# The first step's preparation without the queued walks, and the last image's ending eight pieces wide

## The chip, the core and the metric

The kernel runs on one core of one Trainium2 chip. Each core has five engines with their own instruction streams: PE (TensorE, matmuls, with PEld its weight loads), DVE (VectorE), ACT (ScalarE), POOL (GpSimd) and SP (SyncE), which here issues every DMA. Engines wait for one another by semaphores. An engine works through its own stream strictly in the order in which the program was written, so an instruction that waits holds back everything behind it on that engine. The metric is the device time of one execution in microseconds (us), the median over several runs.

## What is computed

The input is eight images of 64 x 64 positions with 96 channels. Every image passes through a selective-scan block, a linear attention and a small quantised network:

```
x = x + ss2d(group_norm(x))            # per image
    xz = x @ in_proj ; 3x3 depthwise conv + silu -> xc ; z is the gate
    xs = xc read along two diagonal orders, forwards and backwards (4 directions)
    delta = softplus(...) ; h_t = h_{t-1} * exp(delta_t * A) + delta_t * u_t * B_t ; y_t = h_t . C_t   # 16 states
    y = the four directions put back in place and added ; layer norm ; * silu(z) ; @ out_proj
t = t + attention(layer_norm(t))       # without softmax: one 97 x 97 Gram matrix per image is enough
t = t + ffn(layer_norm(t))             # 96 -> 384 -> 96, operands rounded to 8 bits
```

## The kernel before

**The scan loop.** `run` walks through 128 sections: 8 images, two passes each (`q` 0 forwards, 1 backwards), and 8 sections of 512 positions (`T`) per pass. A section has 16 states, so the main loop has 2048 steps, one section and state each. In one step ACT makes `decay` (L966) and the scaled input `feedT` (L980), PE turns it into `feed` in PSUM (L988, or L990), DVE scans three groups into `h` (L1001), POOL copies the carry (L1017) and multiplies `h` by C (L1022), and PE adds the result into `y` four steps later (L1036). The row of C for a step is a DMA `cc<-crow` (L957), issued four steps ahead into one of five buffers.

**The prologue of a section.** `prologue(m)` makes what the 16 steps of a section need: matmuls from `u` (L878), `rows` (L883), its transpose and `x` (L888, L891), three matmuls with absolute value (L901, L903), exponential and logarithm (L905, L908), four POOL passes (L912 to L917), three matmuls and DVE passes (L920, L922), `du` on POOL (L929), and its transposes and copies (L934, L936). Sections after the first have it spread over the steps of the section before.

**What is put between the steps.** Everything else is written as generators that hand back an engine and an estimated time, and class `Work` places them: `at(tag)` is called at fixed places in a step and lets jobs put instructions into that engine's stream until a credit is used up. Prologues are urgent; the others are jobs, drawn from streams of phases with a width (how many pieces are open at once). `finish(enough)` runs the same machine without a scan loop beside it, until a condition holds. In it every open job moves on by one engine's worth per round, in the order A, V, P, G.

Per image the phases are: `measures` (group norm statistics, 8 pieces), `front` (fetch and norm, L411 to L506; convolution, L536; the `walk` pieces, which read the stored image along the diagonals, L581, transpose, L588, copy, L590, and store the sequence, L593), and after the scans `tail`. `front` of the next image and `tail` of the previous image are placed between the scan steps. Two stretches have no scan beside them:

- *the start*: `finish` runs until the weights are loaded and walks 0 and 1 of the first image are stored; then `bring` loads `u` for two sections, `prologue(0)` is started, and `finish(lambda: not work.urgent)` runs until it is placed. That call places waiting walks too.
- *the end*: after the last step, `tail` of the last image.

**The ending `tail`.** It has three phases. `join`, 8 pieces of 512 positions: load the two directions `y0`, `y1`, the input and the gate (L625, L627, L632); add the two directions on PE with identity matmuls (L640); copy and take statistics (L647, L650, L651); `rsqrt` (two small ACT and seven small POOL instructions); normalise on ACT (L656); transpose and multiply by the gate (L662, L664); out-projection (L668 to L679); copy (L683), store to `mid` (L684), statistics again, normalise on POOL (L695), Gram matrix (L701), transpose (L712), copy and store to `turned` (L715, L717). Then `attention`, one short chain of 97-wide matmuls (L728 to L746). Then `layers`, 8 pieces: load `xaT` and `t` back (L760, L762), matmuls (L765, L770), copy and statistics (L774, L778), normalise on POOL (L785), transpose (L790), three 8-bit matmuls with two ACT passes each (L799 to L802), L805, L810, L815, two POOL additions (L818, L819) and the store (L820). `join` and `layers` run three pieces at a time.

**PSUM and SBUF.** PSUM's eight banks are: three `feed`, two `bank` for the jobs, and `y` over three. When the loop is over the jobs also have the `feed` banks. The scans' SBUF buffers come from one pool that stays open to the end.

Of the kernel before, what the change touches and what calls it, by code (L numbers as in the profile page):

```python
# [13 lines left out]
ALU = mybir.AluOpType  # L14
# [36 lines left out]
@with_exitstack  # L51
def hybrid_block(ctx, tc, x, out, w):


    nc = tc.nc
    NB = x.shape[0]
    const = ctx.enter_context(tc.tile_pool(name="const", bufs=1))
    dram = ctx.enter_context(tc.tile_pool(name="dram", bufs=4, space=DRAM))
    k = weights(tc, const, dram, w)
    pool = ctx.enter_context(tc.tile_pool(name="scan", bufs=1))  # L60
    psum = ctx.enter_context(tc.tile_pool(name="psum", bufs=1, space=PSUM))
    with tc.manual_schedule():

        k.tables = lambda: nc.scalar.preload_act_table_set("natural_log_exp_and_others")
        run(tc, pool, psum, dram, x, out, k, NB)


def weights(tc, const, dram, w):
# [57 lines left out]

    dd = tile("dd", [P, 2, G])
    both = tile("both", [P, G])
    logs = tile("logs", [P, ND, NJ])
    turned = tile("turned", [ND * NJ, P])  # L130

    def loads():

        nc.sync.dma_start(out=logs, in_=w["a_logs"])
# [24 lines left out]
        nc.scalar.copy(turned, v)  # L159
        k.release(ps)  # L160
        rows = dram.tile([ND * NJ, P], F32, tag="logs", name="logs")
        nc.sync.dma_start(out=rows, in_=turned)
        yield SPIN
        for q in range(2):
            for d in range(2):
                for g in range(G):
                    j = (2 * q + d) * NJ + g * (GC // DPT)
                    nc.sync.dma_start(
                        out=k.a_neg[d * GC : (d + 1) * GC, q, g, :],
                        in_=rows[j : j + GC // DPT, :].rearrange("j (i n) -> (j i) n", n=NS),  # L170
                    )
            yield SPIN
# [18 lines left out]
    def layers():  # L191
# [18 lines left out]
        with tc.tile_pool(name="prep", bufs=1, side="right") as prep:  # L210
            w1s = load("w1s", [DM, HID], w["w1"], pool=prep)
            w2s = load("w2s", [P, 3, DM], w["w2"], pool=prep)
            b1s = load("b1s", [P, 3], w["b1"], pool=prep)
# [5 lines left out]
            nc.vector.tensor_copy(k.w1q, w1s, saturate=False)  # L219
            nc.vector.tensor_copy(k.w2q, w2s, saturate=False)  # L220
# [44 lines left out]
class Work:  # L265
# [6 lines left out]
    def __init__(self, banks):  # L272
        self.now = 0
        self.alone = False
        self.urgent, self.jobs, self.streams = [], [], []
        self.free = [(b, -9) for b in banks]
        self.kept = []
        self.long = []
        self.credit = dict.fromkeys(self.PLACES, 0.0)

# [39 lines left out]
    def at(self, tag, place=0):  # L320
        gain, most = self.PLACES[tag]
        self.credit[tag] = min(most, self.credit[tag] + gain)
        for j in self.urgent + self.jobs:
            while not j.done and j.tag == tag:
                if j.ready > (self.now, place) and (j.spin or not self.alone):
                    break
# [42 lines left out]
    def finish(self, enough):  # L369
# [6 lines left out]
        self.alone = False  # L376
        self.credit = dict.fromkeys(self.PLACES, 0.0)


def view(b, p, *dims):  # L380

# [24 lines left out]
    return r, m  # L406


def fetched(nc, pool, x, b, c):
    xt = pool.tile([P, 4, DM], F32, tag="xt", name="xt", bufs=2)  # L410
    nc.sync.dma_start(out=xt, in_=x[b].rearrange("(t p) c -> p t c", p=P)[:, 4 * c : 4 * c + 4, :])  # L411
    return xt

# [54 lines left out]
def front(tc, work, x, k, at, b):  # L468
# [8 lines left out]
    with tc.tile_pool(name=f"f1_{b}", bufs=1, **area) as p1, tc.tile_pool(name=f"f2_{b}", bufs=2, **area) as p2:  # L477
# [16 lines left out]

        def norm(c):

            xt = fetched(nc, p2, x, b, c)
            ps = yield bank(0.45, 4)
            v = channels(nc, k, ps, xt)
            yield act(0.65)  # L500
            nc.scalar.activation(
                xp[0:DM, 1 + 8 * c : 9 + 8 * c, 1 : WW + 1], v.rearrange("p (h w) -> p h w", w=WW),
                AF.Identity, scale=at.norm[:, 0:1], bias=at.norm[:, 1:2],
            )
            work.release(ps)
            normed.add(c)  # L506
# [92 lines left out]
        yield [walk(c) for c in range(NST)], 3  # L599


def tail(tc, work, x, out, k, at, b):

    nc = tc.nc
    area = dict(reuse_waits="tile")
    with tc.tile_pool(name=f"t1_{b}", bufs=1, **area) as p1:
        gram = p1.tile([DM + 1, DM + 1], F32, tag="gram", name="gram")
        grams = [0]

        with tc.tile_pool(name=f"t2_{b}", bufs=2, **area) as p2:  # L610

            joined = set()

            def join(c):
                s = slice(4 * c, 4 * c + 4)

                def tile(name, shape, bufs=2):
                    return p2.tile(shape, F32, tag=name, name=name, bufs=bufs)
# [7 lines left out]
                t = tile("t", [P, 4, DM], 3)  # L626
                nc.sync.dma_start(out=t, in_=x[b].rearrange("(t p) c -> p t c", p=P)[:, s, :])  # L627
                yield "P", 0.0, 4, False
                while c >= 2 and c - 2 not in joined:
# [3 lines left out]
                st, mv = tile("st", [P, 4, 6]), tile("mv", [P, 4, 2])  # L633
                yn = ys[0]
                for j in range(2):
# [21 lines left out]
                yg = tile("yg", [HC, 2, CH])  # L657
                for a in range(2):
                    ps = yield bank(0.45)
                    v = view(ps, HC, CH)  # L660
# [20 lines left out]
                        )  # L681
                yield act(0.5)
                nc.scalar.copy(t, po)  # L683
                nc.sync.dma_start(out=at.mid[:, s, :], in_=t)  # L684
                yield dve(1.7, 0)
                for i in range(4):
                    nc.vector.bn_stats(st[:, i, :], po[:, i, :])
# [25 lines left out]
                xaT = ys[1].rearrange("p a c -> p (a c)")[0 : DM + 1, 0:CH]  # L713
                yield act(0.6)
                nc.scalar.copy(xaT, v)  # L715
                work.release(ps)
                nc.sync.dma_start(out=at.turned[:, c * CH : (c + 1) * CH], in_=xaT)  # L717
                joined.add(c)

            yield [join(c) for c in range(NCH)], 3  # L720

        att = SimpleNamespace()

# [24 lines left out]

        yield [attention()], 1

        with tc.tile_pool(name=f"t3_{b}", bufs=3, **area) as p2:

            def layers(c):
                s = slice(4 * c, 4 * c + 4)
# [4 lines left out]
                xaT = tile("xaT", [DM + 1, CH])  # L759
                nc.sync.dma_start(out=xaT, in_=at.turned[:, c * CH : (c + 1) * CH])  # L760
                t = tile("t", [P, 4, DM])
                nc.sync.dma_start(out=t, in_=at.mid[:, s, :])  # L762
# [56 lines left out]
                nc.gpsimd.tensor_tensor(t, t, y16, ALU.add)  # L819
                nc.sync.dma_start(out=out[b].rearrange("(t p) c -> p t c", p=P)[:, s, :], in_=t)  # L820

            yield [layers(c) for c in range(NCH)], 3


def run(tc, pool, psum, dram, x, out, w, NB):

# [4 lines left out]


    nc = tc.nc
    steps = [
        (b, q, c) for b in range(NB) for q in range(2) for c in (range(NST) if q == 0 else range(NST - 1, -1, -1))
    ]
# [281 lines left out]
    for m in range(2):  # L1120
        bring(m)
    work.start(prologue(0), urgent=True)
    work.finish(lambda: not work.urgent)

    work.kept = feed
    work.finish(lambda: all(any(f is x for x, _ in work.free) for f in feed))
# [17 lines left out]
    for i in range(total + LAG + 1):  # L1144
# [34 lines left out]
        if i + 4 < total:  # L1179
            fetch(i + 4)  # L1180
        feeds.pop(i, None)
    work.free += [(f, -9) for f in feed]
    work.kept = []
    work.stream(end(NB - 1))
    work.finish(all_done)


# [75 lines left out]
```

## Time and profile before

| | us |
|---|---|
| median of 3 runs | 12009.75 (12005.47 to 12027.36) |
| profiled execution, its own time | 12015.44 |
| its span, first to last instruction | 12013.6 |
| first scan instruction (L1001) starts | 308.18 |
| first load of the last image's ending (L625) is issued | 11640.26 |
| busy: PE, DVE, ACT, POOL | 9964.7, 9683.0, 9500.1, 9739.2 |

The busy times are totals over the span. All four engines are busy for about four fifths of it, but not alike everywhere: the first 308 us and the last 373 us have no scan in them, and they must be read on their own. In a line of the timeline the columns are start, duration from the first to the end of the last merged instruction, engine, line, operation, output and input, count, and in brackets the idle time before it with what ended it. In a line of the chain of waits they are start, duration and what was running or being waited for.

### The profile page before, as it was taken

What the parts mean: (1) busy time and instruction counts of PE and PEld (TensorE: products, weight loads), DVE (VectorE), ACT (ScalarE), POOL (GpSimd) and SP (SyncE); (2) the same over time, 40 slices, a digit from 0 to 9 for tenths busy, and PEclk for the clock granted to TensorE, in tenths of its full rate; (3) what the DMA queues carried; (4) which work ended last, traced back from release to release, by engine and by line L of the source; (5) the groups of instructions that cost most, each with busy time, mean ns of one, the idle gap of its engine ahead of it and who ended that gap; (6) DMA issues with size and microseconds to landing.
All of it is one profiled execution on the core that took longest, in us unless ns stands there. A gap on an engine that the chain in (4) does not pass through costs nothing.

```text
span 12013.6 us, 186895 instructions
## 1 busy us (share of the span) xinstructions
PE 9964.7 (83%) x62805; PEld 8013.1 (67%) x62805; DVE 9683.0 (81%) x11092; ACT 9500.1 (79%) x19843; POOL 9739.2 (81%) x6927
## 2 busy tenths in 40 slices
PE   5888889888898888888898888988889888888875
PEld 4676677666676667766676666766667666666653
DVE  1888988888888888888888888888888878888971
ACT  2888888878887788887888778887788878878862
POOL 0879988889878888788988888878898888889972
PEclk8999999998999989999899999989899998988985
DMA  3234333533335333343334433343333533322331
GB/s 98 84 97 129 100 91 89 136 106 101 88 96 143 98 93 95 107 125 103 91 92 128 116 93 90 95 129 109 96 92 92 134 105 94 105 83 82 99 96 39
DMA packets 1126629, 1213.55 MB, mean 101 GB/s; under 512 B 453061, under 2 KB 732326, under 8 KB 1125670
## 3 DMA queue, kind: packets, MB, share of 16 engines
q1 hardware_dynamic: 1125670, 1201.61, 36.4%
q8 instruction: 499, 8.18, 0.3%
q14 instruction: 460, 3.77, 0.1%
HBM read 877.99 MB, written 323.14 MB: 100 GB/s over the span
## 4 chain that ended last, share of the span: by engine, by line
PE 30%; ACT 20%; DVE 20%; POOL 12%; issue 9%; DMA 4%; SPq 3%; DVEq 0%; POOLq 0%; ACTq 0%
DVE h L1001 13%; ACT feedT L980 8%; PE y L1036 7%; PE feed L988 7%; POOL h L1022 7%; ACT decay L966 6%; DVE feed L1005 4%; PE bank L536 3%; DMA cc<-crow 2%; PE bank L878 2%; SPq L581 2%; POOL delta L917 1%; PE bank L920 1%; PE feed L990 1%; PE bank L901 1%
## 5 line engine op out<-in xcount | busy, mean ns | idle before, releaser
L1022 POOL TENSOR_TENSOR h<-h,cc 128x1536 f32<-128x1536 f32 x2048 | 7073.5, 3454 | 390.0 <-DMA cc<-crow 197.1
L1001 DVE TENSOR_TENSOR_SCAN h<-decay,carry,feed 128x512 f32<-128x512 f32 x5376 | 6502.6, 1261 | 635.1 <-PE feed L988 528.8
L966 ACT ACTIVATE decay<-delta,a_neg 128x512 f32<-128x512 f32 x6144 | 3976.2, 713 | 1287.5 <-DVE h L1001 1281.8
L988 PE MATMUL feed<-ident,feedT 128*128 128x128 f32 x15360 | 2746.2, 303 | 1502.8 <-DVE h L1001 1211.3
L1036 PE MATMUL y<-ident,h 128*128 128x128 f32 x24576 | 3806.0, 290 | 72.2 <-ACT ys L1064 40.2
L980 ACT ACTIVATE feedT<-duT,rows 128x192 f32<-128x192 f32 x10240 | 3671.1, 443 | 4.5 <-PE feed L988 3.9
L1036 PEld LDWEIGHTS y<-ident,h 128*128 128x128 f32 x24576 | 3151.0, 151 | 530.5 <-issue 477.3
L988 PEld LDWEIGHTS feed<-ident,feedT 128*128 128x128 f32 x15360 | 1972.3, 155 | 2121.2 <-DVE h L1001 663.5
L1005 DVE TENSOR_TENSOR feed<-feed,du 128x512 f32<-128x512 f32 x2304 | 1442.1, 686 | 209.7 <-PE feed L990 205.2
L1017 POOL COPY carry<-h 128x3 f32<-128x3 f32 x2048 | 395.7, 193 | 1072.5 <-DVE h L1001 959.6
L1001 DVE TENSOR_TENSOR_SCAN h<-decay,feed 128x512 f32<-128x512 f32 x768 | 883.3, 1201 | 95.5 <-PE feed L988 80.4
L536 PE MATMUL bank<-wf,xp 97*128 97x192 f32 x4266 | 864.6, 334 | 1.2 <-DVE delta L922 1.2
L990 PE MATMUL feed<-x,pick 77*128 77x512 f32 x1536 | 848.6, 635 | 0.6
L536 PEld LDWEIGHTS bank<-wf,xp 97*128 97x128 f32 x4266 | 696.0, 195 | 29.6 <-issue 18.5
L922 DVE SCALAR_TENSOR_TENSOR delta<-bank,delta 128x512 f32<-128x512 f32 x383 | 259.7, 678 | 280.8 <-POOL delta L917 144.7
L929 POOL TENSOR_TENSOR du<-delta,u 128x1536 f32<-128x1536 f32 x128 | 449.6, 3513 | 36.1 <-DVE delta L922 36.1
L920 PE MATMUL bank<-x,ws 13*128 13x512 f32 x766 | 444.9, 661 | 17.6 <-DVE delta L922 17.6
L915 POOL TENSOR_TENSOR e<-e,duT 128x1536 f32<-128x1536 f32 x128 | 441.7, 3451 | 14.5 <-ACT delta L908 14.4
L901 PE MATMUL bank<-x,ws 13*128 13x512 f32 x764 | 434.1, 648 | 15.0 <-ACT x L891 15.0
L917 POOL TENSOR_TENSOR delta<-delta,e 128x1536 f32<-128x1536 f32 x128 | 441.2, 3447 | 0.1
L912 POOL TENSOR_SCALAR duT<-e 128x1536 f32<-128x1536 f32 x128 | 193.9, 1514 | 227.8 <-ACT e L905 227.8
L990 PEld LDWEIGHTS feed<-x,pick 77*128 77x128 f32 x1536 | 261.4, 202 | 153.7 <-issue 97.7
(263 smaller groups left out, 9059.9 us busy)
## 6 DMA issues: line engine op xcount, KB each, us to landing
cc<-crow SPq DMA_DIRECT2D x4096, 128.0 KB
u<-seq SPq DMA_DIRECT2D x256, 384.0 KB
wide<-ys SPq DMA_DIRECT2D x512, 192.0 KB
ut<-image SPq DMA_DIRECT2D x768, 64.0 KB
seq<-us SPq DMA_DIRECT2D x128, 384.0 KB
part<-ys SPq DMA_DIRECT2D x64, 768.0 KB
y<-part SPq DMA_DIRECT2D x64, 768.0 KB
y<-wide SPq DMA_DIRECT2D x256, 192.0 KB
```

The costliest lines, as they stand in the source:

```text
L536: nc.tensor.matmul(v[:, j, :], flat[:, o : o + P], k.wf[:, i, :], start=(i == 0), stop=(i == 8), skip_group_check=True)
L901: nc.tensor.matmul(ps, w.ws[:, q, g, :], x[0 : 2 * NR + 1, :], start=True, stop=True)
L917: nc.gpsimd.tensor_tensor(delta, delta, e, ALU.add)
L920: nc.tensor.matmul(ps, w.ws[:, q, g, :], x[0 : 2 * NR + 1, :], start=True, stop=True)
L966: nc.scalar.activation(decays[i][:, g, :], made[m].delta[:, g, :], AF.Exp, scale=w.a_neg[:, q, g, n : n + 1])
L980: nc.scalar.activation(f[part], o.duT[part], AF.Copy, scale=scale)
L988: nc.tensor.transpose(feed[g][:, j * P : (j + 1) * P], feeds[i][:, j * G + g, :], w.ident)
L990: nc.tensor.matmul(feed[0], w.pick[:, FEED[:n].count("D"), :], made[m].x, start=True, stop=True)
L1001: nc.vector.tensor_tensor_scan(h[:, g, back], a[:, g, back], feed[g][:, back], init, ALU.mult, ALU.add)
L1005: nc.vector.tensor_tensor(feed[g], feed[0], made[m].du[:, g, :], ALU.mult)
L1022: nc.gpsimd.tensor_tensor(hs[i], hs[i], c.unsqueeze(1).to_broadcast([P, G, T]), ALU.mult)
L1036: nc.tensor.matmul(y[:, j, :], hs[i][:, g, r * P : (r + 1) * P], w.ident, is_transpose=True, start=(n == 0 and j % 4 == 0), stop=(n == NS ...
```

## The change

It has four parts.

1. A new method `hurry` replaces `finish` for `prologue(0)`: only urgent jobs are placed, and no new pieces are drawn from the streams. Walks 3 to 7 of the first image come later, among the scan steps.
2. The last image's `tail` is called with `last=True`, after the scans' SBUF pool has been closed and the three banks of `y` have been added to the free banks. All phases are eight pieces wide. The two directions are added by one DVE instruction of 128 x 768 instead of PE; the PE additions and the ACT copy after them fall away for this image. `t` and `xaT` stay in SBUF, so the stores to `mid` and `turned` and the loads from them fall away.
3. `norm` in `front` fetches into three buffers instead of two (`measures` keeps two).
4. Some weight tiles move into short-lived memory, and the two bias loads `b1s`, `b2s` are issued after the first three walks' loads instead of before them.

```
@@ class Work
-        for j in self.urgent + self.jobs:
+        for j in self.urgent + ([] if self.hurried else self.jobs):
...
+    def hurry(self, enough):
+        self.alone = self.hurried = True
+        while not enough():
+            self.now += 1
+            for tag, place in (("A", 0), ("V", 0), ("P", 2), ("G", 0)):
+                self.at(tag, place)
+        self.alone = self.hurried = False
@@ norm in front
-            xt = fetched(nc, p2, x, b, c)
+            xt = fetched(nc, p2, x, b, c, 3)
@@ tail
-        with tc.tile_pool(name=f"t2_{b}", bufs=2, **area) as p2:
+        with tc.tile_pool(name=f"t2_{b}", bufs=8 if last else 2, **area) as p2:
...
+                t = p1.tile([P, 4, DM], F32, tag=f"t{c}", name="t") if last else tile("t", [P, 4, DM], 3)
...
+                if last:
+                    yield dve(2.5)
+                    nc.vector.tensor_tensor(yn, ys[0], ys[1], ALU.add)
+                    for i in range(4):
+                        nc.vector.bn_stats(st[:, i, :], yn[:, i, :])
+                        nc.vector.bn_aggr(mv[:, i, :], st[:, i, :])
+                for j in range(0 if last else 2):
...
-                nc.sync.dma_start(out=at.mid[:, s, :], in_=t)
+                if not last:
+                    nc.sync.dma_start(out=at.mid[:, s, :], in_=t)
...
-                nc.sync.dma_start(out=at.turned[:, c * CH : (c + 1) * CH], in_=xaT)
+                if last:
+                    kept[c] = t, xaT
+                else:
+                    nc.sync.dma_start(out=at.turned[:, c * CH : (c + 1) * CH], in_=xaT)
...
-            yield [join(c) for c in range(NCH)], 3
+            yield [join(c) for c in range(NCH)], 8 if last else 3
@@ layers
+                if last:
+                    t, xaT = kept[c]
...
-            yield [layers(c) for c in range(NCH)], 3
+            yield [layers(c) for c in range(NCH)], 8 if last else 3
@@ run
     work.start(prologue(0), urgent=True)
-    work.finish(lambda: not work.urgent)
+    work.hurry(lambda: not work.urgent)
...
-    work.free += [(f, -9) for f in feed]
+    work.finish(all_done)
+    scans.close()
+    y = psum.tile([P, TB * G, P], F32, tag="y", name="y_end").rearrange("p (b k) c -> p b (k c)", b=G)
+    work.free += [(f, -9) for f in feed] + [(y[:, g, :], -9) for g in range(G)]
     work.kept = []
-    work.stream(end(NB - 1))
+    work.stream(tail(tc, work, x, out, w, image(NB - 1), NB - 1, True))
     work.finish(all_done)
```

More of the change, by code (lines that the diff above doesn't have):

```diff
@@ L59, in hybrid_block @@
     k = weights(tc, const, dram, w)
-    pool = ctx.enter_context(tc.tile_pool(name="scan", bufs=1))
     psum = ctx.enter_context(tc.tile_pool(name="psum", bufs=1, space=PSUM))
@@ L64, in hybrid_block @@
         k.tables = lambda: nc.scalar.preload_act_table_set("natural_log_exp_and_others")
-        run(tc, pool, psum, dram, x, out, k, NB)
+        run(tc, psum, dram, x, out, k, NB)
 def weights(tc, const, dram, w):
@@ L128, in weights, with transfers @@
     both = tile("both", [P, G])
-    logs = tile("logs", [P, ND, NJ])
-    turned = tile("turned", [ND * NJ, P])
     def loads():
+        with tc.tile_pool(name="prep", bufs=1, side="right") as prep:
+            yield from transfers(tile("logs", [P, ND, NJ], pool=prep), tile("turned", [ND * NJ, P], pool=prep))
+    def transfers(logs, turned):
         nc.sync.dma_start(out=logs, in_=w["a_logs"])
@@ L212, in layers @@
             w2s = load("w2s", [P, 3, DM], w["w2"], pool=prep)
+            for _ in range(2):
+                yield SPIN
+            nc.vector.tensor_copy(k.w1q, w1s, saturate=False)
+            nc.vector.tensor_copy(k.w2q, w2s, saturate=False)
+        with tc.tile_pool(name="prep", bufs=1, side="right") as prep:
             b1s = load("b1s", [P, 3], w["b1"], pool=prep)
@@ L217, in layers @@
                 yield SPIN
-            nc.vector.tensor_copy(k.w1q, w1s, saturate=False)
-            nc.vector.tensor_copy(k.w2q, w2s, saturate=False)
             s8 = tile("b1e", [P, 3], F8, prep)
@@ L277, in __init__ @@
         self.kept = []
+        self.hurried = False
         self.long = []
@@ L406, in rsqrt, with fetched @@
     return r, m
-def fetched(nc, pool, x, b, c):
-    xt = pool.tile([P, 4, DM], F32, tag="xt", name="xt", bufs=2)
+def fetched(nc, pool, x, b, c, bufs=2):
+    xt = pool.tile([P, 4, DM], F32, tag="xt", name="xt", bufs=bufs)
     nc.sync.dma_start(out=xt, in_=x[b].rearrange("(t p) c -> p t c", p=P)[:, 4 * c : 4 * c + 4, :])
@@ L599, in front, with tail @@
         yield [walk(c) for c in range(NST)], 3
-def tail(tc, work, x, out, k, at, b):
+def tail(tc, work, x, out, k, at, b, last=False):
     nc = tc.nc
@@ L608, in tail @@
         grams = [0]
-        with tc.tile_pool(name=f"t2_{b}", bufs=2, **area) as p2:
+        kept = {}
+        with tc.tile_pool(name=f"t2_{b}", bufs=8 if last else 2, **area) as p2:
             joined = set()
@@ L617, in tile @@
                 def tile(name, shape, bufs=2):
-                    return p2.tile(shape, F32, tag=name, name=name, bufs=bufs)
+                    return p2.tile(shape, F32, tag=name, name=name, bufs=8 if last else bufs)
                 ys = [tile(f"y{d}", [P, 4, DI], 3) for d in range(2)]
@@ L625, in join @@
                         nc.sync.dma_start(out=y[v * WW : (v + 1) * WW], in_=rv)
-                t = tile("t", [P, 4, DM], 3)
+                t = p1.tile([P, 4, DM], F32, tag=f"t{c}", name="t") if last else tile("t", [P, 4, DM], 3)
                 nc.sync.dma_start(out=t, in_=x[b].rearrange("(t p) c -> p t c", p=P)[:, s, :])
-                yield "P", 0.0, 4, False
-                while c >= 2 and c - 2 not in joined:
+                if not last:
+                    yield "P", 0.0, 4, False
+                while not last and c >= 2 and c - 2 not in joined:
                     yield SPIN
@@ L633, in join @@
                 st, mv = tile("st", [P, 4, 6]), tile("mv", [P, 4, 2])
+                yg = tile("yg", [HC, 2, CH]) if last else None
                 yn = ys[0]
-                for j in range(2):
+                if last:
[5 more added lines that the diff above has]
+                for j in range(0 if last else 2):
                     ps = yield bank(0.65)
@@ L656, in join @@
                     nc.scalar.activation(yn[:, i, :], yn[:, i, :], AF.Identity, scale=r[:, i : i + 1], bias=m[:, i : i + 1])
-                yg = tile("yg", [HC, 2, CH])
+                yg = yg or tile("yg", [HC, 2, CH])
                 for a in range(2):
@@ L683, in join @@
                 nc.scalar.copy(t, po)
-                nc.sync.dma_start(out=at.mid[:, s, :], in_=t)
+                if not last:
+                    nc.sync.dma_start(out=at.mid[:, s, :], in_=t)
                 yield dve(1.7, 0)
@@ L712, in join @@
                     nc.tensor.transpose(v[:, i * P : (i + 1) * P], xa[:, i, :], k.ident)
-                xaT = ys[1].rearrange("p a c -> p (a c)")[0 : DM + 1, 0:CH]
+                if last:
+                    xaT = p1.tile([DM + 1, CH], F32, tag=f"xaT{c}", name="xaT")
+                else:
+                    xaT = ys[1].rearrange("p a c -> p (a c)")[0 : DM + 1, 0:CH]
                 yield act(0.6)
@@ L716, in join @@
                 work.release(ps)
-                nc.sync.dma_start(out=at.turned[:, c * CH : (c + 1) * CH], in_=xaT)
+                if last:
+                    kept[c] = t, xaT
+                else:
+                    nc.sync.dma_start(out=at.turned[:, c * CH : (c + 1) * CH], in_=xaT)
                 joined.add(c)
-            yield [join(c) for c in range(NCH)], 3
+            yield [join(c) for c in range(NCH)], 8 if last else 3
         att = SimpleNamespace()
@@ L749, in tail @@
         yield [attention()], 1
-        with tc.tile_pool(name=f"t3_{b}", bufs=3, **area) as p2:
+        with tc.tile_pool(name=f"t3_{b}", bufs=8 if last else 3, **area) as p2:
             def layers(c):
@@ L757, in tile @@
                     return p2.tile(shape, dtype, tag=name, name=name)
[L759 to L762, printed above, removed]
+                if last:
+                    t, xaT = kept[c]
+                else:
+                    xaT = tile("xaT", [DM + 1, CH])
+                    nc.sync.dma_start(out=xaT, in_=at.turned[:, c * CH : (c + 1) * CH])
+                    t = tile("t", [P, 4, DM])
+                    nc.sync.dma_start(out=t, in_=at.mid[:, s, :])
                 ps = yield bank(0.65, 4)
@@ L820, in layers, with run @@
                 nc.sync.dma_start(out=out[b].rearrange("(t p) c -> p t c", p=P)[:, s, :], in_=t)
-            yield [layers(c) for c in range(NCH)], 3
-def run(tc, pool, psum, dram, x, out, w, NB):
+            yield [layers(c) for c in range(NCH)], 8 if last else 3
+def run(tc, psum, dram, x, out, w, NB):
     nc = tc.nc
+    scans = ExitStack()
+    pool = scans.enter_context(tc.tile_pool(name="scan", bufs=1))
     steps = [
```

## The prediction

> **What bounds the kernel now.** I read first the busy time in three stretches (until the first scan, the loop, after it), then the timeline of the start, the chain of waits at the end, and last the SP queue's waits. The stretches (us; busy time and count for PE, PEld, DVE, ACT, POOL; clock; DMA):
>
> ```profile
> 0.00:308.00 308.00, 177.39 (x917) 149.80 (x917) 46.66 (x122) 69.02 (x88) 22.31 (x28) 0.81 0.40 100
> 308.00:11634.00 11326.00, 9598.31 (x61086) 7719.44 (x61086) 9572.21 (x10739) 9351.44 (x19575) 9641.64 (x6642) 0.92 0.37 103
> 11634.00:12014.00 380.00, 189.04 (x802) 143.86 (x802) 64.14 (x232) 79.63 (x182) 75.24 (x257) 0.58 0.20 54
> ```
>
> In the loop four engines share 83 to 85% each: nothing there is to be had cheaply. In the last 380 us nothing is busy for more than half: that stretch is latency. The start shows the same, in the timeline from 220 us:
>
> ```profile
> 220.59 5.37 PE L878 MATMUL feed<-wx,u 128*128 128x77 f32 x24 [15.91 <-DMA u<-seq]
> 226.00 0.41 ACT L883 COPY rows<-feed 128x308 f32<-128x308 f32 x1 [20.36 <-PE feed L878]
> ...
> 244.58 1.06 PE L888 MATMUL feed<-ident,rows 128*77 128x128 f32 x4
> ...
> 261.22 3.41 POOL L917 TENSOR_TENSOR delta<-delta,e 128x1536 f32<-128x1536 f32 x1
> 268.32 1.09 PE L588 MATMUL feed<-ident,ut 128*128 128x128 f32 x4 [16.01 <-DMA ut<-image]
> ...
> 279.02 2.07 PE L920 MATMUL feed<-x,ws 13*128 13x512 f32 x2
> ```
>
> The transpose of `rows` could follow at 226.4 and runs at 244.58, because PE's stream has walk transposes ahead of it that wait for `ut`; the same happens between L917 (ends 264.6) and L920 (279.0). In the chain of waits at the end, transfers through memory stand out:
>
> ```profile
> 11736.87 10.16 DMA turned<-y
> ...
> 11852.33 17.67 DMA t<-mid
> ...
> 11914.68 16.94 DMA t<-mid
> ...
> 11967.74 17.29 DMA t<-mid
> ```
>
> **Start.** What is left of the first prologue, with its own durations. The bias load `b2s` holds SP (the chain has 8.32 us for it and SP's 36 `ut` issues take 26.7 us instead of 36 x 0.66 = 23.8); moved behind the walks, that and its own two issues (0.9) bring `u` about 3.6 us earlier, so L878 starts at 217. Then 5.4 (L878), 0.5 (L883), 1.1 and 0.8 (L888, L891), 3 x 1.04 and a copy, 3.8 (L901, L903), 1.5 (L905), 10.0 (POOL, L912 to L917), 2.3 (DVE, L922; its matmuls no longer queue behind walks), 3.5 (L929), 3 x 1.1 (L934; L936 lies beside it), 5.3 and 0.5 (L878 and L883 of the next section, ahead of L966 on ACT), 3.8 from the first L966 to the first scan: 217 + 41.8 = 259. All PE figures are those of half clock. Before it was 308.2. **Gain 49.** The weight tiles' new place costs nothing: its few DVE copies (0.2 to 0.4 each) lie under the walks' loads; without that cover, 2.
>
> The five walks left out (3 to 7) go among the first 20 steps: 60 transposes (x 0.27 = 16 us PE), 15 copies (8.7 us ACT), on SP 60 `ut` issues and 10 `seq` stores that wait for those copies with `cc` loads behind them. The built program shows that SP issues the first 36 behind the `cc` loads of steps 0 to 3, so they run at 235 to 262 under the prologue, ahead of their transposes; the other 24 (16 us) stand before the `cc` load of step 12, which has about 25 us of lead. The measures and convolution of image 1 also move 41 steps later, into steps that had nothing. What a walk costs in the loop is seen in image 1: POOL's L1022 counts 22 steps in 900 to 1000 us, with walks, and 22 in 1200 to 1300, without. So nearly nothing; at the other end all of its ACT and PE time, 25. Nearest row: nothing; but the first steps run at a lower clock (0.83 in 300 to 400), so I take **6**. If POOL or `cc` gave no cover, it is 25.
>
> **Norm's third buffer.** SP's waits in 1600 to 1700, the same in every later front:
>
> ```profile
> SPq L411 <- PE bank L418: 24.8, 1, 24.8
> ```
>
> The third fetch waits for the first piece's transposes, and `cc` loads queue behind it; POOL then waits 7.6 to 9.3 us for `cc` (9.3 in this window), in six images, 51 in sum. With three buffers this goes. But the chain of waits through 1664 to 1684 runs over PE and DVE while POOL stands, and over the whole run PE waited 26 us for L1022: the adding into `y` lies three steps behind. Between 0 and 51 I take **a gain of 6**.
>
> **End.** The built program keeps the eight pieces in lockstep: each engine does one phase for all eight, then the next. ACT's stream has the eight logarithms first and then the eight normalisations, so nothing is normalised before the last piece has landed. From the first load at 11640.3:
>
> - Loads: 786 KB of y, 197 of t, 393 of gate, x 8 = 11.0 MB. The three-piece burst at 11645 to 11655 moved 222 to 236 GB/s at a full DMA share: 49 us, to 11690. (48 issues x 0.66 = 32 on SP are hidden by that.)
> - DVE on the last piece: the new addition, 128 x 768. L1005 has 0.69 for 512 and L706 0.23 for 97: 0.97 by that slope (bounds 0.69 and 1.4); four pairs of statistics at 0.5. 3 us, then L396, L397: to 11693.5. The other seven lie under the loads.
> - ACT normalises, 32 x 0.476 (eight L656 took 3.81): 15.2, to 11708.7.
> - PE: second half of the transposes, 32 at 1.09 for four (half clock, L588) would be 8.7, at full clock 4.3: 6, to 11715.
> - Out-projection, see below: 38, to 11753. Copies and statistics lie under it but for the last three (their banks are one tile, and the first copy waits for all three): 2, to 11755.
> - POOL, `rsqrt` and L695: 3.72 a piece in the trace, 29.8, to 11785.
> - Last Gram, 32 transposes, copy, and `attention` (11830.8 to 11836.0): 12.6, to 11797.5.
> - L765 and L770: 3.3 a piece at half clock, half that at full: 20, plus 1, to 11818.5.
> - POOL, `rsqrt` and L785: 3.71 x 8 = 29.7, to 11848; 1.5 to the first L801.
> - ACT L801 and L802: 1.23 a pair, 24 pairs, 29.5, to 11879. L805 and L810 (1.14 a piece) lie under it.
> - L815, then POOL L818 and L819, 1.86 a piece: 15.4, to 11894.5; last store as before, 3.2, to 11897.7.
>
> Against 12013.6: **gain 116**. Gone are L640 (37.6 us of PE), L647, and all transfers over `mid` and `turned`. What is late next is POOL twice and ACT twice, 104 us together, then PE.
>
> The out-projection's size hangs on PE's clock. The row (start and end, length, five busy times, clock):
>
> ```profile
> 11804.00:11824.00 20.00, 19.36 (x80) 17.14 (x81) 2.70 (x10) 3.25 (x8) 3.05 (x13) 0.50 0.03 10
> ```
>
> PE was busy for 19.4 of 20 us with this very work and stayed at half clock: 8.1 us a piece, 65 for eight. At 11668 to 11676 the same work ran at full clock, 4.35 a piece, 35. The Trainium skill, page "TensorE: Matmul & The Clock Gate", Part 1, says that about 3.4 us of sustained work lifts the gate: by that rule, 35. The trace contradicts it for these narrow matmuls begun cold; but it also shows runs of transposes and of 192-wide matmuls warm within 3 to 4 us (11682 to 11686, 11740 to 11744), and in the new order 32 transposes come straight before. So I take 38 and keep 65.
>
> **Sum.** -49 + 6 - 6 - 116 = -165. The profiled execution (12015.44) is 5.7 above the median of 12009.75 and inside the runs shown; the differences apply to both: 12009.75 - 165 = 11845.
>
> **Rivals.**
> - *The out-projection stays cold.* For it: the row above. Against: the transposes ahead of it. +27: 11872.
> - *The walks take back what the start gave.* For it: in 308 to 400 us a step takes 5.4 us against 4.5 later, so the first steps may have no room. Against: image 1. +19 on my sum (25 for 6); with late `cc` loads up to all of the 49 gained: 11864 to 11888.
> - *SP's 24 us wait was on the path.* Then all 51 come back, 45 more than in my sum: 11800.
> - *The lockstep doesn't come about* (a wait on reused memory puts the pieces in a row). The built program's waits show only loads, the last `h` and the last sums ahead of the pieces. I give it no share of its own.
> - *Slower: the scan pool may now lie elsewhere in SBUF.* POOL, DVE and ACT read and write it in every step. From 0.08 us a step on, 2048 steps eat all 165; at 0.1 (205 us) the time is 12050. Against: L1022 keeps within 3415 and 3488 ns over all its buffers, and the order of the steps from image 2 on is the same in both programs.
>
> **How the numbers follow.** My forecast 0.74, cold out-projection 0.11, walks 0.05, SP wait 0.05, slower 0.03. The 0.2% that a measurement of this kernel can tell is 24 us, so all but the last are clearly faster; shortfalls that add up to no change have 0.02. Range: down to 11802 (nearly all of the SP wait), up to 11898 (cold matmuls and some 26 from the walks or slower loads). Faster 0.95, same 0.02, slower 0.03.
>
> **What would show it.** First scan at about 259 us, with L888 directly behind L883; some 17 steps in the first 92 us after it; no SP wait over 5 us on norm's third fetch, POOL's wait for `cc` down from 197 to about 150; ending 255 to 260 us from the first y load, no `mid` or `turned` in its chain, the first L656 some 50 us after the first y load, two POOL stretches of 30 us each, clock over 0.9 in the out-projection. A first scan after 275, an ending over 300, or a loop longer by 40 would make it wrong.

## The result and the profile after

The changed kernel takes 11833.3 us (median; runs from 11827.4 to 11837.3), the kernel before on the same chip 12016.1. The ratio is 0.9847, 95% interval 0.9831 to 0.9862: faster by about 1.5%. The profiled execution took 11827.4 us, with a span of 11825.6, 188.0 shorter than the span before. The forecast was 11845. Part of that nearness comes from the starting point: the forecast was worked out from 12009.75, the median known then. In differences, 165 us less were forecast, 183 were measured by the medians and 188 by the profiled executions.

Two marks cut the span into three parts: the first scan, and the first load of the last ending. Here and below, the times are those of profiled executions.

| part | before | after | difference | forecast |
|---|---|---|---|---|
| start, to the first scan | 308.2 | 255.5 | -52.7 | -49 |
| loop, first scan to first y load | 11332.1 | 11324.9 | -7.2 | 0 (+6 - 6) |
| ending, first y load to the end | 373.3 | 245.2 | -128.1 | -116 |

The three stretches of the kernel after, in the columns used for the kernel before:

```profile
0.00:255.50 255.50, 163.90 (x833) 138.17 (x833) 42.32 (x116) 60.73 (x74) 22.31 (x28) 0.84 0.37 93
255.50:11573.00 11317.50, 9593.98 (x61168) 7730.79 (x61169) 9576.45 (x10744) 9358.49 (x19589) 9640.72 (x6642) 0.92 0.37 103
11573.00:11826.00 253.00, 124.62 (x678) 89.31 (x676) 69.45 (x240) 70.52 (x166) 74.75 (x257) 0.62 0.27 56
```

The loop is about as busy as before. The ending keeps its DVE, ACT and POOL work (69, 71 and 75 us, against 64, 80 and 75) in 253 us instead of 380, and PE has lost 64 us of work. It is still mostly latency: no engine is busy for half of it.

The start, in the timeline. L915, L920, L925, L957 and L954 are the old L878, L883, L888, L920 and L917:

```profile
214.76 5.38 PE L915 MATMUL feed<-wx,u 128*128 128x77 f32 x24 [15.78 <-DMA u<-seq]
220.17 0.41 ACT L920 COPY rows<-feed 128x308 f32<-128x308 f32 x1 [20.23 <-PE feed L915]
220.64 1.13 PE L925 MATMUL bank<-ident,rows 128*77 128x128 f32 x4 [0.51 <-ACT rows L920]
...
229.28 23.69 SPq L595 DMA_DIRECT2D ut<-image  x36
...
229.53 3.62 PE L957 MATMUL bank<-x,ws 13*128 13x512 f32 x4
...
236.94 3.41 POOL L954 TENSOR_TENSOR delta<-delta,e 128x1536 f32<-128x1536 f32 x1
```

The transpose of `rows` now follows its copy at once, where PE had left it for 18 us behind the walks' transposes, and the matmuls of L957 are done before POOL is, where they had come 14 us after it. The walks' 36 loads are still issued here, but nothing on PE waits for them any more. The first scan starts at 255.54. That is at the low end: of the twelve kernels of this study that start with `hurry`, ten have their first scan between 258.3 and 259.8, and two at 255.1 and 255.5, with the same start in the program. So one profile tells the start to some 4 us.

The ending, in the chain of waits (start, duration, what ran or was waited for):

```profile
11590.41 7.11 DMA y<-wide
...
11622.20 7.99 DMA y<-wide
11630.39 0.97 DVE y L656
...
11634.40 3.52 PE bank L687 x8
...
11654.02 0.65 PE bank L693 x2
...
11683.54 0.67 PE y_end L693 x2
...
11691.25 1.64 POOL y L721 x4
...
11728.53 1.58 PE feed L800 x2
...
11752.19 1.64 POOL xf L820 x4
...
11778.96 0.72 ACT h L837
...
11809.35 0.92 POOL y L853
```

There is no `mid` and no `turned` in it. The chain goes from one engine to the next: loads, ACT and PE, PE, POOL, PE, POOL, ACT, POOL.

### The profile page after: what moved, and what is told of

Its sections match the earlier page's. It is cut to its first block, busy times and chain, and to the rows that moved or that the text cites. A ratio compares the mean times of both kernels' runs of the same rounds, so it can differ in the third digit from the quotient of the medians.

```text
span 11825.6 us, 186556 instructions
## 1 busy us (share of the span) xinstructions
PE 9882.5 (84%) x62677; PEld 7958.3 (67%) x62677; DVE 9688.2 (82%) x11100; ACT 9489.7 (80%) x19827; POOL 9737.8 (82%) x6927
## 4 chain that ended last, share of the span: by engine, by line
PE 33%; DVE 21%; ACT 20%; POOL 11%; issue 8%; DMA 4%; SPq 3%; DVEq 0%; POOLq 0%; ACTq 0%
DVE h L1038 13%; PE y L1073 8%; PE feed L1025 8%; ACT feedT L1017 7%; POOL h L1059 6%; ACT decay L1003 5%; DVE feed L1042 5%; PE bank L550 4%; DMA cc<-crow 2%; PE bank L915 2%; PE bank L957 2%; SPq L595 2%; PE feed L1027 1%; POOL delta L954 1%; PE bank L938 1%
## 5 line engine op out<-in xcount | busy, mean ns | idle before, releaser
L959 DVE SCALAR_TENSOR_TENSOR delta<-bank,delta 128x512 f32<-128x512 f32 x383 | 259.8, 679 | 257.6 <-PE bank L957 136.1
L966 POOL TENSOR_TENSOR du<-delta,u 128x1536 f32<-128x1536 f32 x128 | 449.6, 3513 | 14.1 <-DVE delta L959 14.1
L954 POOL TENSOR_TENSOR delta<-delta,e 128x1536 f32<-128x1536 f32 x128 | 441.1, 3446 | 0.1
L957 PE MATMUL bank<-x,ws 13*128 13x512 f32 x766 | 440.9, 656 | 0.0
```

What stands on the lines that cost most here:

```text
L954: nc.gpsimd.tensor_tensor(delta, delta, e, ALU.add)
L957: nc.tensor.matmul(ps, w.ws[:, q, g, :], x[0 : 2 * NR + 1, :], start=True, stop=True)
```

## The experiments

Eight kernels of this study share the changed kernel's loop, instruction for instruction (the changed kernel, and the five below whose edits lie in the ending, and two later ones). Their loops, first scan to first y load, took 11313.3 to 11338.4 us, 11328.7 on average with a standard deviation of 7.6. That is what one profile can tell of a loop. Five kernels share its ending in the same way: 243.3 to 249.0 us.

### Norm's third buffer

Edit:

```
-            xt = fetched(nc, p2, x, b, c, 3)
+            xt = fetched(nc, p2, x, b, c)
```

> The changed kernel with norm's fetch in two buffers again; nothing else differs. Against the changed kernel (11833 us): by the prediction's step the third buffer is worth 6 us, so 11839, inside what a measurement can tell. Rival, from the two traces: the lead of the scans grows from about 35 us at the second image to 60 us at the last; if that is the third buffer's work, this kernel takes 11858 and its lead stays at about 35 us. Both expect the waits of 24 us on the fetch to come back.

Measured: 11865.3 us (ratio to the kernel before 0.9874, interval 0.9860 to 0.9887; the changed kernel has 0.9847). Its loop takes 11359.3 us, 31 more than the mean of the eight. The forecast's 6 us was wrong. What SP and POOL wait for in the 120 us around the third image's front (us in total, times, longest):

```profile
SPq L425 <- PE bank L432: 25.5, 1, 25.5
```

```profile
POOL h L1059 <- DMA cc<-crow: 9.2, 1, 9.2
```

In the changed kernel, at the same front, SP's longest wait on L425 is 0.6 us and POOL does not wait for `cc`.

So far this is a correlation. Is it SP's wait, or that the third piece comes earlier? The next kernel keeps three buffers and puts only the wait back (`small` and `late` have two buffers, as `norm`'s pool has by default):

```
             xt = fetched(nc, p2, x, b, c, 3)
+            if b and c < 3:
+                small = p2.tile([P, 1], F32, tag="small", name="small")
+                late = p2.tile([P, 1], F32, tag="late", name="late")
+                nc.sync.dma_start(out=small, in_=x[b][0:P, 0:1])
...
             yield act(0.65)
+            if b and c < 3:
+                nc.scalar.copy(late, small)
```

> The changed kernel with norm's fetch in three buffers, and a wait of the old kind put back beside it: from the second image on, each of the first three pieces also fetches one column of the input into a tile with two buffers, which ACT copies (once per piece, unused) just ahead of its normalisation. The third of these small fetches holds SP until the first piece reaches ACT, some 25 us, while the pieces themselves have come early. If the third buffer gains through SP (cc loads no longer queue behind a waiting fetch), this kernel is as slow as the one with two buffers: 11860 to 11868, with the waits of 8 to 9 us on cc back at each front. If it gains because the third piece comes earlier, this kernel stays at 11833 to 11838.

Measured: 11856.0 us (ratio 0.9859, interval 0.9842 to 0.9875), loop 11354.4, 26 above the mean of the eight. Around the second image's front, SP and POOL wait again:

```profile
SPq L515 <- ACT late L520: 23.0, 1, 23.0
```

```profile
POOL h L1065 <- DMA cc<-crow: 7.6, 1, 7.6
```

(The small fetches and copies themselves are in the 26 us too.)

A third kernel went the other way, with two buffers but no wait: from the second image on, a piece is fetched only after the piece two before it has been read.

```
+            while b and c >= 2 and c - 2 not in normed:
+                yield SPIN
             xt = fetched(nc, p2, x, b, c)
```

> The kernel with two buffers in norm (11865 us, against 11833 with three), but from the second image on a piece of norm is fetched only once the piece two before it has been read, so that no fetch waits in SP's stream for the first piece's transposes. If the two buffers cost what they cost through SP (the cc loads queue behind the waiting fetch and POOL waits 8 to 9 us for cc at each front), this kernel comes to 11833 to 11840 and those waits are gone. If the pieces of norm being late is the cost itself, it stays at 11860 or more.

Measured: 11797.7 us (11781.6 to 11811.0; ratio 0.9813, interval 0.9799 to 0.9826), below the changed kernel, which neither theory expected. Its loop takes 11292.5 us. SP no longer waits over 2 us for norm's fetch after the start.

What each kernel loses at the fronts can be counted, because every step has three scans (steps are counted from 0 in each image, 256 to an image). In images 2 to 7 of the eight (there are six such fronts) the pieces of `norm` for the next image are fetched between step 9 and step 47, and with the wait POOL's missed row falls into step 16. The time from the first scan of step 16 to that of step 48, and the sum over the six fronts against the changed kernel:

| kernel | buffers | SP waits about 24 us | steps 16 to 48, us | six fronts, us |
|---|---|---|---|---|
| before | 2 | yes | 179.4 to 180.4 | +32.6 |
| changed | 3 | no | 173.9 to 175.5 | 0 |
| two buffers | 2 | yes | 179.4 to 180.5 | +33.8 |
| wait put back | 3 | yes | 179.7 to 181.1 | +35.0 |
| fetched late | 2 | no | 174.7 to 178.4 | +5.4 |

The other seven kernels with the changed loop lie between +1.4 and +3.2. So the cost goes with SP's wait, and not with the number of buffers or with an early third piece: 4 to 7 us at each front, some 34 us in all. The path shows in the waits of DVE (in total, times, longest), from 1900 to 11500 us, first in the changed kernel and then with two buffers:

```profile
DVE delta L959 <- POOL delta L954: 111.4, 20, 13.7
```

```profile
DVE delta L959 <- POOL delta L954: 139.1, 27, 13.7
```

A fetch that waits 24 us holds the `cc` rows behind it in SP's stream, and POOL misses one row for 8 to 9 us. POOL's passes for the next section's prologue (up to L954) come late by that, and L959, which stands in DVE's stream ahead of later scans, waits for them. At each of the six fronts DVE has one such wait of 5.0 to 5.8 us in the kernel before, in the one with two buffers and in the one with the wait put back, and none in the changed kernel or in the one with the late fetch.

The rest of what the late fetch gains lies elsewhere. By the count of scans it is about 2 us ahead of the two-buffer kernel at step 64 of image 2, 10 at step 128, 21 at step 192 and 39 at step 240, and gives 26 of these back by step 16 of image 3. Walks and tail, which follow `norm`, come some 3 to 15 steps later in it. What that placement saves was not tested by a kernel of its own; what the traces show is that DVE's wait on L954 falls from 151 to 99 us over the whole run. They show too that in the changed kernel POOL waits 9.1 to 10.1 us for `cc` at step 207 or 208 of images 2 to 7, each time shortly after SP stood 5.4 to 6.3 us behind a load `xaT<-turned`, and that these six waits of POOL are gone with the late fetch.

### The walks

```
-    work.hurry(lambda: not work.urgent)
+    work.finish(lambda: not work.urgent)
```

> The changed kernel with finish in place of hurry for the first prologue, so that all waiting walks are placed ahead of the first scan again. Against the changed kernel (11833 us): by the prediction, start 49 later less 6 for walks out of the loop, so +43, 11876. Rival, from the traces (first scan 52.6 earlier, lead of the scans down from 53 to about 35 us by the second image): walks in the loop cost 18, so +35, 11868. In both, the first scan starts at 303 to 308 us, a little earlier if the later bias loads alone bring u forward.

Measured: 11870.9 us (ratio 0.9873, interval 0.9860 to 0.9887). The first scan starts at 302.3, so `hurry` is worth 42 to 47 us of the start (the ten kernels and the changed one), and the later bias loads, which this kernel keeps, are worth 5.9 give or take 4. Its loop takes 11317.1 us, 12 less than the mean of the eight: walks among the steps cost 12 us, give or take the 8 of one profile, where the forecast had 6 and the rival 18. Counted by scans from each kernel's first, the loss lies in the first image: up to step 16 of the second, this kernel's loop is 12.7 us ahead of the changed kernel's, and that of the kernel before 17.9. POOL's wait for `cc` goes with it: 0.3 us up to 1600 us here, 29 us in the changed kernel.

### The ending as before, with the free banks

```
-    work.stream(tail(tc, work, x, out, w, image(NB - 1), NB - 1, True))
+    work.stream(tail(tc, work, x, out, w, image(NB - 1), NB - 1))
```

> The changed kernel with the last image's ending as before (three pieces wide, additions on PE, transfers over mid and turned), but still with the three banks of y free and the scan's memory closed. Against the changed kernel (11833 us): prediction +116, traces +128, so 11949 to 11961, with a first y load to the end of 373 us. Rival: the additional banks and memory carry part of the gain by themselves, then clearly less than +116.

Measured: 11982.4 us (ratio 0.9966, interval 0.9954 to 0.9978), ending 389.3. That is 16 more than the kernel before has with five banks. Eight free banks and the scans' memory bring nothing by themselves; why the old ending is longer with them was not followed.

### Addition on PE

```
-                if last:
-                    yield dve(2.5)
-                    nc.vector.tensor_tensor(yn, ys[0], ys[1], ALU.add)
...
-                for j in range(0 if last else 2):
+                for j in range(2):
```

> The changed kernel, but in its eight-wide ending the two directions are added by identity matmuls on PE with the ACT copy after them, in place of the DVE addition. By the prediction's reasoning seven of eight pieces hide under the 50 us of loads and the last costs 4.7 us of PE (37.6 us over eight) and a copy or two: +6 to +9, 11839 to 11842. Rival: PE at half clock can't hide it, all 37.6 us stand in the chain: 11871. A third possibility: PE is warmer at the transposes and the out-projection, and nothing or less than nothing is lost: 11828 to 11833.

Measured: 11846.1 us (ratio 0.9851, interval 0.9837 to 0.9864), ending 258.3: +13.1. In lockstep more than the last piece is left when the last load has landed: the chain has 70 of the 128 matmuls of this line from 11638.8 to 11652.6, 13.8 us, where the DVE addition has 0.97. So the expectation's "seven of eight pieces hide" was too many, and the rival's "all 37.6 us stand in the chain" too few.

### Transfers or width

Two kernels take the two halves of the new ending apart. The first is eight wide but goes through memory again (stores to `mid` and `turned`, loads of `xaT` and `t`); the second keeps `t` and `xaT` but is three wide:

```
-            yield [join(c) for c in range(NCH)], 8 if last else 3
+            yield [join(c) for c in range(NCH)], 3
...
-            yield [layers(c) for c in range(NCH)], 8 if last else 3
+            yield [layers(c) for c in range(NCH)], 3
```

> The changed kernel, eight wide, with the transfers over mid and turned put back: the stores after the copies and the loads in front of the layers. Read from the first y load to the end of the span, 245 us in the changed kernel and 373 before. Theory (the lockstep of eight is what pays: a transfer's latency of some 17 us is met once for all eight pieces and not once a group): +17 to +25, 262 to 270 us. Rival (the transfers themselves are what was saved): half or more of the 128 us comes back, 310 us or more.

> The changed kernel with t and xaT kept in memory and the addition on DVE, but join and layers three pieces wide. Read from the first y load to the end of the span (245 us in the changed kernel, 373 before). Theory (the width pays most): 310 to 340 us, since PE goes back to half clock in groups of three and the latencies of a piece's chain are met three times. Rival (the transfers were what was saved): 270 us or less.

Measured, one execution each: through memory 11948.3 us, ending 357.6 (+112); three wide 11834.3 us, ending 242.8 (-2). The theory (the width pays) falls on both: with the transfers gone the width gives no gain, and the transfers alone bring 112 of the 128 us back. The SP queue in the eight-wide kernel with transfers (start, duration, line, count; the last six of the eight stores, then the loads), and 10 us of it (busy times, clock, DMA share, GB/s):

```profile
11730.72 44.89 SPq L745 DMA_DIRECT2D turned<-xaT  x6
...
11785.51 7.35 SPq L791 DMA_DIRECT2D t<-mid  x1
11793.03 0.52 SPq L789 DMA_DIRECT2D xaT<-turned  x1
11793.60 7.52 SPq L791 DMA_DIRECT2D t<-mid  x1
```

```profile
11758.00:11768.00 10.00, 0.00 (x0) 0.00 (x0) 0.00 (x0) 0.00 (x0) 0.00 (x0) 0.50 0.07 26
```

While every engine stands still, the stores to `turned` run at 26 GB/s with a DMA share of 0.07, about one sixteenth, which is one DMA engine of 16 at work. 194 KB then take 7.5 us. The loads of `xaT` have the same shape (11785 to 11793 us: again 26 GB/s at 0.07), and SP stands about as long at each `t` load queued behind one. Eight stores and eight loads at 7.5 us are 120 us, about the 112 that came back. The shape fits a rule of the Trainium skill, page "DMA: Bandwidth & Descriptors", section "Why a DMA increments its semaphore by 16 and not by 1": a transfer is shared among the largest number of engines, up to 16, that divides the slowest dimension on both of its sides. `turned` has 97 rows, a prime, so one engine; `y`, with 64 rows a load, moved 231 GB/s at a share of 1.15 (11590 to 11600 us in the changed kernel). The gate's loads are the nearest comparison, 96 rows in pieces of the same 2 KB: their 3.15 MB landed with all other loads within 50 us, where 26 GB/s would have taken 121. That another row count would cure `turned` itself was not tried.

### A cold out-projection

```
+                if last:
+                    yield act(20.0)
+                for _ in range(20 if last and c == 0 else 0):
+                    nc.scalar.copy(yg, yg)
                 ps = yield bank(0.65)
```

> The changed kernel with 20 additional ACT copies of the first piece's gated tile in front of its out-projection, so that PE stands still for some 12 to 15 us between the transposes and the eight out-projections (33.8 us in the changed kernel, begun warm). If this work stays at half clock whenever it begins cold (as the slice of the kernel before shows), the out-projection takes 65 us and the ending grows by the pause and 31, about 290 us. If 3 to 4 us of work are enough to lift the clock, it takes 34 to 38 us and the ending grows by the pause alone, about 260 us.

Measured, one execution: 11888.8 us, ending 292.3. The out-projection, 10 us in its middle, first in the changed kernel and then here (PE and PEld busy first, the clock third from the right):

```profile
11660.00:11670.00 10.00, 10.00 (x84) 9.47 (x84) 3.26 (x19) 0.96 (x2) 0.19 (x1) 1.00 0.00 0
```

```profile
11690.00:11700.00 10.00, 10.00 (x45) 9.39 (x45) 1.44 (x8) 0.48 (x1) 0.19 (x1) 0.50 0.00 0
...
11730.00:11740.00 10.00, 10.00 (x45) 9.39 (x44) 0.00 (x0) 0.00 (x0) 0.00 (x0) 0.50 0.00 0
```

PE is busy for 10.00 of 10 us in both. Begun warm, it runs 84 matmuls in that time at full clock and 4.2 us a piece; begun cold, 45 at half clock and 8.1 a piece, 64 us in all without ever warming up. The ending grew by 47.1 us, about 30 of it from the clock and the rest from the pause. What lifts the clock in the changed kernel is not PE's busy share either: while ACT paced the transposes, from 11638 to 11648 us, PE was busy throughout and the clock stayed at 0.50; in the run of transposes without pauses that followed (11648.4 to 11654.0) it went to 1.00 after 4 us.

### Two better endings

POOL's two stretches given to DVE (`rsqrt`, L721 and L820 on `nc.vector` for the last image):

> The changed kernel with POOL's two stretches of the ending (seven small instructions and four scalings a piece, 3.71 us each, 29.7 us a stretch) given to DVE, which stands idle there. DVE's 128x97 addition takes 0.23 us, so 7 x 0.1 and 4 x 0.23 = 1.6 us a piece, 13 a stretch: the ending should fall by 34 us, from 245 to 211. If something else ends those stretches just behind POOL (ACT's logarithms, PE), less than 15 us come back.

Measured, one execution: ending 234.7, so 10 us less and not 34: the second outcome named ahead (under 15 us). The 128x4 instructions take 0.16 us, not 0.1, and a scaling 0.33, so a piece takes 2.22 us. And POOL had begun its stretch while DVE was still at the statistics; on DVE the two stand one behind the other.

A stagger, each piece starting two rounds behind the one before it:

```
+                for _ in range(2 * c if last else 0):
+                    yield SPIN
```

(in `join` behind the loads, in `layers` at the top)

> The changed kernel with each piece of join and of layers started two rounds of the scheduler behind the one before it, so that the engines work on different pieces at once instead of passing all eight from one engine to the next. By the busy times of the ending (POOL 75, ACT 70, DVE 69, PE 125 us, of 253) no engine needs more than half of the stretch if PE stays warm: 190 to 215 us for the ending against 245. If PE falls back to half clock because its work comes in bits, the out-projection alone takes 65 us again and the ending stays at 235 to 260.

Measured, one execution: 11765.5 us, ending 178.4, 67 less and below the 190 to 215 expected. Three slices, each with PE, PEld, DVE, ACT, POOL, clock, DMA:

```profile
11620.00:11630.00 10.00, 8.53 (x70) 7.84 (x70) 5.46 (x20) 3.91 (x11) 4.69 (x16) 1.00 1.16 219
11630.00:11640.00 10.00, 8.25 (x55) 7.22 (x55) 5.47 (x20) 3.24 (x9) 7.34 (x23) 0.83 0.88 164
11640.00:11650.00 10.00, 7.41 (x61) 6.38 (x59) 6.99 (x29) 5.12 (x15) 6.72 (x23) 1.00 0.01 2
```

Four engines work at once, partly still under the loads, where the changed kernel mostly had one. PE's clock lies between 0.75 and 1.00 from 11615 to 11675 us, the stretch with the out-projections, and between 0.50 and 0.83 after it.

Both edits that gained, the late fetch and the stagger, together:

> The changed kernel with the two edits that gained most put together: norm's pieces fetched late into two buffers (11798 us alone) and join and layers started in a stagger (11765 us alone, ending 178 us against 245). If the two don't touch, 11833 - 35 - 67 = 11731, with an ending of 178 us. If the late pieces gained by an accident of the interleaving, 11760.

Measured: 11732.4 us (11727.8 to 11758.2; ratio 0.9762, interval 0.9748 to 0.9775), as the sum had it. Its profile is of the slowest of the five executions (11758.2; ending 184.8). It is faster than either edit alone (11797.7 and, from one execution, 11765.5).

## Why the prediction was right

The total came within 12 us and each of the three parts within about 12, but not every step held, and the loop's total came out by luck. By the prediction's own steps:

- *Start, -49; measured -52.7.* With ten of the twelve kernels that start with `hurry` it is -48 to -50: the forecast's first scan at 259 is theirs, and the -52.7 is within what one profile tells. From L915 to the first scan the forecast had 41.8 us; the changed kernel took 40.8. Single terms were off within that: PE was assumed at half clock throughout, and the second section's 24 matmuls of L915 took 2.9 us, not 5.3.
- *Walks in the loop, +6.* It measures 12 +- 8 in one profile, and 13 to 18 counted over the first image, so two to three times the forecast. The bound of 25, all of their ACT and PE time, was not reached.
- *Norm's third buffer, -6.* **This step failed.** The rows were read rightly (24.8 us of SP, 7.6 to 9.3 us of POOL), but the gain was cut to 6 because the chain of waits in one window ran over PE and DVE, and because PE hardly waits for L1022. It measures 31 +- 8 by the loop and 33 to 34 counted at the fronts, about two thirds of POOL's 51 us. What was left out is the other way from POOL to the scans: its passes for the prologue, for which DVE waits. The page of the kernel before has it (busy and mean, then the idle time before L922 and what ended most of it):

```profile
L922 DVE SCALAR_TENSOR_TENSOR delta<-bank,delta 128x512 f32<-128x512 f32 x383 | 259.7, 678 | 280.8 <-POOL delta L917 144.7
```

A chain shows what ended each wait in one place; it does not show that the delay of another engine is absorbed later. The rival ("then all 51 come back") was given 0.05 and was nearer than the forecast.
- *The loop as a whole, 0; measured -7,* or -3 by the mean of the eight. That is luck: two terms were much too small and have opposite signs. Counted by scans against the kernel before, the changed kernel loses 17.9 us up to step 16 of image 2, gains 32.6 at the six fronts, and loses 7 in all other steps, where kernels with the same loop differ by more than that.
- *Ending, -116; measured -128.* Stage by stage, from the first y load:

| stage | forecast | measured |
|---|---|---|
| loads, to the last y | 49.7 | 49.9 |
| addition, statistics, to the first L681 | 3.5 | 3.5 |
| ACT normalises | 15.2 | 14.1 |
| second half of the transposes | 6.3 | 6.1 |
| out-projection | 38 | 33.8 |
| copies and POOL to the last L721 | 32.0 | 31.1 |
| Gram, transposes, attention | 12.5 | 9.6 |
| layers on PE, then POOL to the last L820 | 50.5 | 47.6 |
| first matmuls, 24 pairs on ACT | 31 | 30.5 |
| last additions and store | 18.7 | 19.0 |
| sum | 257.4 | 245.2 |

The lockstep was read from the program, and single durations from the rows before; nearly all of it holds to about 1 us. Ten of the 12 us lie in three rows with PE in them (out-projection, Gram, layers): its clock was better than assumed.

- *The clock.* The choice of 38 against 65 was right for the reason given, that transposes come straight before; the kernel with the pause shows the other state. The rule of the Trainium skill, page "TensorE: Matmul & The Clock Gate", Part 1 (some 3.4 us of sustained work lift the gate), gives 35 and is right for the changed kernel, begun warm (33.8). It does not hold for the same work begun cold, with PE busy for 64 us and the clock at 0.50 throughout.
- *What the sum did not need to know.* "Gone are L640, L647, and all transfers": it did not say which of these carried the gain. It was the transfers (by the rates above mainly the 97-row ones), and neither the width nor (but for 13 us) the DVE addition.
- *SBUF placement, the slower rival:* the eight loops, 11328.7 us on average, are no longer than the loop before, 11332.1.

Of the signs named ahead, SP's wait on norm's fetch is gone after the start, POOL's wait for `cc` fell from 197 to 175 and not to 150 (the walks brought 29 us of new waits), and POOL's two stretches take 30 us each.

## What to carry to other kernels

A wait in a queue that feeds the main loop can cost more than the chain of waits in one window suggests; here it was 6 us forecast and some 34 measured. Put a number on it by the time that the same steps take with and without it, and look for every engine that waits for the one held up, not only for the one that the chain happens to name. Where an ending is latency, look first at what a transfer moves per us: a slow shape (here 97 rows, 26 GB/s) can cost more than any stage of arithmetic around it, and it can hold a queue in the main loop too. And once the transfers are gone, try to stagger the pieces rather than pass all of them from engine to engine; here that was worth 67 us of 245.

## What the hardware showed

- In these traces stores and loads of 97 rows of 2 KB move 26 GB/s at a DMA share of 0.07, and SP stands some 7.5 us at the issue of a load queued behind them; loads of 64 rows moved 231 GB/s.
- 96-column f32 matmuls with a weight load each kept half clock for 64 us when begun cold, at 10.00 of 10 us busy, and full clock for 33.8 us when begun within 1 us of a run of transposes.
- The same small work differs little between two engines: a scaling of 128x96 in f32 took 0.33 us on DVE and 0.42 on POOL, a 128x4 instruction 0.16 and 0.19. Moving it from POOL to DVE gained 10 us where 34 had been expected.
